# A sparse graph transformer on one core: twenty gathers of each of the last two layers issued during the end of the layer before

## Chip, core and metric

The kernel runs on one core of a Trainium2 chip. The metric is the device time of one launch in microseconds (us), as the median of three runs.

## The reference, cut to what matters

There are 3327 nodes of 256 features and a 0/1 adjacency of 3327 x 3327 with about 16 ones in a row. Layer 0 is one graph attention step; layers 1 to 3 are masked transformer layers of the same form with their own weights:

```python
qkv = layer_norm(x, g1, be1) @ w_qkv
q, k, v = ...                                   # 8 heads of 32
scores = einsum('nhd,mhd->hnm', q, k) * SCALE
scores = where(adj != 0, scores, -inf)
out = einsum('hnm,mhd->nhd', softmax(scores), v).reshape(n, 256)
x = x + out @ w_proj + b_proj
x = x + gelu(layer_norm(x, g2, be2) @ w1 + b1) @ w2 + b2     # 1024 wide
```

## The kernel before, in words

**Layer 0 and the lists.** Layer 0 reads the adjacency once (25 loads of 1.66 MB), sorts the nodes by their number of neighbours, largest first, and keeps for every node the list of its neighbours. The sorted nodes lie in 26 blocks of 128; block 0 has the nodes with the most neighbours. `CAPS` holds the list length of each block: 34 for block 0, 23 for block 1, 12, 12, 11, 10 and 9 for blocks 21 to 25; their sum is 430. `idx` holds the lists, `bias` a large negative number where a list has a place too many.

**A layer.** Keys and values of all nodes lie in DRAM as rows of 512 floats (`kv_dr`; in layer 1 a 513th number is the key's place in the sorted order, which `scores` copies into `idx` for the later layers). The blocks are worked off in `ORDER`: 24, 23, ..., 0, then 25. A block's list is cut into groups of up to four places (`cuts`). For each group:

- `gather` issues one indirect DMA a place on the POOL queue (L767): 128 rows, one for each node of the block, into a buffer (`slots`) of 4 rows of `SLW` floats. There are 12 buffers (`SLOTS`), used in turn.
- `scores` multiplies the keys by q (L781) and sums over each head (L782), on DVE. q stands in PSUM (`place_q`, ACT, L760).
- After a block's last group, `exps` makes the exponentials (L788 to L792), and beside the next block's groups `shares` (L798 to L800) and `values` follow: a DVE multiplication of the values by the shares (L812) and two PE transposes a place that add up in PSUM (L815); then ACT copies the sum to SBUF (L821).

**A tail.** When both blocks of a chunk (`CHUNKS`: 23 and 24, 21 and 22, ..., 1 and 2, then 0 alone, 25 alone) are done, `tail` runs as a generator, one step at a time: the projection (L666, L670), the addition to x (L673) and the variances on DVE; the power -1/2 on POOL (`powers`, L139, tiles rsig); the normalised rows on ACT (xn, L155), their transposes (pn on PE, fT on ACT); two halves of the feed-forward, each a wave of `w1` products (pu, L694), gelu on ACT (L698) and a wave of `w2` products (pd, L707); the second addition (L713). In layers 1 and 2 there follow the next layer's norm (rsig_h, nmu, xn, hT), its qkv products (L185, L190) and the writes of kv and q to DRAM (L729, L730, SP queue). A list `hidden` lets one tail at a time through the feed-forward.

**The order.** `layer` writes the order of all instructions out by hand (`manual_schedule`); each engine and each queue runs its own in that order. The layer is a sequence of turns, one for each group: gathers for up to `AHEAD` = 3 groups further on are issued while a buffer is free, then this group's scores, then `turn()` steps every tail on (twice in a turn of block 25), then some value groups of the block before (`part`; block 1's six are spread over block 0's nine turns by `goal`). After the last block come the remaining values and steps without gathers: I call that stretch the layer's ending. The next layer's first gather waits until all 26 blocks of kv have landed. In layer 3 there is no kv; `write` scatters finished blocks to the output from the POOL queue (L833), and each of these writes waits for the one before.

**A fallback.** After layer 3 a flag is computed from the lists; if it is set, `general` computes everything anew. For the inputs of these runs it is not set.

Of the kernel before, what the change touches and what calls it, by code (L numbers as in the profile page):

```python
# [50 lines left out]
SLW = 2 * D + 16  # L51
# [10 lines left out]
ORDER = list(range(NB - 2, -1, -1)) + [NB - 1]  # L62
CHUNKS = [ORDER[k:k + 2][::-1] for k in range(0, NB - 2, 2)] + [[0], [NB - 1]]


@with_exitstack
def kernel(ctx: ExitStack, tc: tile.TileContext, ins, out: bass.AP):
# [28 lines left out]
    pf = const.tile([P, NB], FP, name="permf")  # L96
    lists = ctx.enter_context(tc.tile_pool(name="lists", bufs=1))
# [140 lines left out]
    with ExitStack() as st:  # L238
# [70 lines left out]
        nc.vector.tensor_copy(pid, pid_i)  # L309
        tri = l0.tile([P, P], BF, name="tri")  # L310
# [205 lines left out]
        def order():  # L516
# [14 lines left out]
            nc.sync.dma_start(kv_dr[1][:, 2 * D:KVW].rearrange("(k p) o -> p (k o)", p=P), rank)  # L531
# [99 lines left out]
    with ExitStack() as st:  # L631
# [25 lines left out]
        def tail(L, w, wqn, blocks, oT):  # L657
# [69 lines left out]
            for j, b in enumerate(blocks):  # L727
                kv, q = qkv_rows(work, gen, wqn, hT[:, :, j * P:(j + 1) * P], L + 1, f"{L + 1}_{b}")
                nc.sync.dma_start(kv_dr[L + 1][b * P:(b + 1) * P, :], kv)  # L729
                nc.sync.dma_start(q_dr[L + 1][:, b, :], q)  # L730
                if j < n - 1:
                    yield 1

        def cuts(b):

            n = -(-CAPS[b] // SG)
            at = [CAPS[b] * k // n for k in range(n + 1)]
            return list(zip(at[:-1], at[1:]))

        class Attend:  # L740


            def __init__(self, L, b):
                self.L, self.b, self.tag, self.S = L, b, f"{L}_{b}", CAPS[b]
                self.cuts = cuts(b)
                self.tiles = []
                self.vdone = 0
                w = qws[ORDER.index(b) % 2]
# [3 lines left out]
            def load_q(self):  # L752
                if self.L == LAYERS[0]:
                    self.q = nodes_[self.b][:, D:2 * D]
                else:
                    self.q = work.tile([P, D], FP, tag="q", bufs=3, name=f"q_{self.tag}")
# [5 lines left out]
            def gather(self, g):  # L762
                a, z = self.cuts[g]
                t = slots.tile([P, SG, SLW], FP, tag="slot", name=f"sl_{self.tag}_{g}")
                w = KVW if self.L == LAYERS[0] else 2 * D
                for k in range(a, z):
                    nc.gpsimd.indirect_dma_start(  # L767
                        out=t[:, k - a, :w], out_offset=None, in_=kv_dr[self.L][:, :],
                        in_offset=bass.IndirectOffsetOnAxis(ap=idx[:, self.b, k:k + 1], axis=0))
                self.tiles.append(t)  # L770

            def scores(self, g):
                a, z = self.cuts[g]
                n = z - a
                if g == 0:
                    self.sc = work.tile([P, LW, HEADS], FP, tag="sc", name=f"sc_{self.tag}")
                if self.L == LAYERS[0]:

                    nc.scalar.copy(idx[:, self.b, a:z], self.tiles[g][:, :n, 2 * D])
                kq = self.tiles[g][:, :n, :D]  # L780
                nc.vector.tensor_mul(kq, kq, self.qp[:, None, :].to_broadcast([P, n, D]))  # L781
# [3 lines left out]
            def exps(self):  # L785
# [6 lines left out]
                nc.scalar.activation(scs, scs, AF.Exp, scale=SCALE)  # L792

# [11 lines left out]
            def values(self, oT, j):  # L805
# [7 lines left out]
                for k in range(n):  # L813
                    for c in range(2):
                        nc.tensor.matmul(self.po[:, c, :], t[:, k, D + c * P:D + (c + 1) * P], ident,  # L815
                                         is_transpose=True, start=False,
                                         stop=(a + k == self.S - 1 and c == 1))
                self.vdone += 1
# [28 lines left out]
        def layer(L):  # L847
# [31 lines left out]
            for k, a in enumerate(att):  # L879
# [3 lines left out]
                for g in range(n):  # L883
# [17 lines left out]
                    if k == NB - 1:  # L901
                        turn()
# [214 lines left out]
```

## Time and profile before

| | us |
|---|---|
| runs: median (lowest, highest) | 2878.28 (2872.93, 2891.91) |
| profiled execution, its own time | 2350.96 |
| its span, first to last instruction | 2349.1 |
| layer 0 and the lists, to the first gather | 0 to 417.8 |
| layer 1: first gather to end of last | 417.8 to 1012.1 |
| ending of layer 1 | 1012.1 to 1086.6 |
| layer 2: first gather to end of last | 1086.6 to 1649.9 |
| ending of layer 2 | 1649.9 to 1724.7 |
| layer 3: first gather to end of last | 1724.7 to 2285.4 |
| last output write starts | 2334.6 |

Mean TensorE clock granted: 0.802 of full speed. The profile is one execution; its times are from the span's start. PE is the matrix engine (PEld its weight loads), DVE the vector engine, ACT the scalar engine, POOL GpSimd, SP the queue of the plain DMAs. A row of a group names line, engine, operation, out<-in, count, busy time, mean ns of one, and the idle time before it with what ended it. A row in order of time names start, length, the instruction, and in brackets the engine's idle time before it and what ended that; "issue" means that nothing the profile shows was waited for.

### The profile page before, as it was taken

To read this page: it belongs to the slowest core of one execution; us is meant where nothing else is said; L and a number is where in the kernel's file an instruction comes from. 1 tells how busy PE (TensorE), PEld (TensorE's weight loads), DVE (VectorE), ACT (ScalarE), POOL (GpSimd) and SP (SyncE) were. 2 spreads that over 40 slices of the span, in tenths; PEclk is the share of its full clock that TensorE was granted. 3 is DMA by queue.
4 is the path that set the end of the run, shared out by engine and by line. 5 is a ranking of instruction groups with operands and counts; after the bars stand their busy time and mean duration, and the time that the engine had idled before them with its cause. 6 is when DMAs were issued, how large, how long until landed. Compare 5 with 4: busy or idle time off the path is not lost. (4 is left out here: it accounts for less than half of the span.)

```text
span 2349.1 us, 26111 instructions
## 1 busy us (share of the span) xinstructions
PE 1619.5 (69%) x8346; PEld 1278.3 (54%) x8346; DVE 1758.5 (75%) x3214; ACT 778.9 (33%) x1564; POOL 1430.9 (61%) x1614
## 2 busy tenths in 40 slices
PE   7676763258767778774578778777837767766666
PEld 6555642146645556553466566655625656554555
DVE  4876774699888888862888878778548888887772
ACT  3876751124333322222134332222321323211112
POOL 1222232777777776723777777767157777777772
PEclk9888886579877778887789877877967888767778
DMA  5767715777777777725777777767167777776761
GB/s 191 253 184 193 193 59 98 203 207 219 234 217 214 218 220 206 211 68 191 217 220 225 230 219 224 233 201 214 46 204 214 211 214 212 212 204 200 203 196 36
DMA packets 165083, 453.05 MB, mean 193 GB/s; under 512 B 37711, under 2 KB 64985, under 8 KB 161609
## 3 DMA queue, kind: packets, MB, share of 16 engines
q0 software_dynamic: 107104, 350.26, 51.8%
q1 hardware_dynamic: 56652, 98.53, 13.5%
q10 hardware_dynamic: 1180, 2.49, 0.4%
q8 instruction: 69, 1.13, 0.2%
q14 instruction: 78, 0.64, 0.1%
HBM read 410.86 MB, written 40.29 MB: 192 GB/s over the span
## 5 line engine op out<-in xcount | busy, mean ns | idle before, releaser
L767 POOL DMA_INDIRECT sl<-kv,idx x1290 | 1228.6, 952 | 410.4 <-issue 311.7
L815 PE MATMUL po<-ident,sl 128*128 128x128 f32 x2580 | 465.7, 344 | 505.2 <-DVE sl L812 479.3
L815 PEld LDWEIGHTS po<-ident,sl 128*128 128x128 f32 x2580 | 393.0, 179 | 568.4 <-DVE sl L812 557.0
L781 DVE TENSOR_TENSOR sl<-sl,qw 128x1024 f32<-128x1024 f32 (+1 forms) x354 | 396.4, 1120 | 170.9 <-DMA sl<-kv,idx 86.8
L782 DVE TENSOR_REDUCE sc<-sl 128x32 f32<-128x1024 f32 (+1 forms) x354 | 398.2, 1125 | 12.1
L812 DVE TENSOR_TENSOR sl<-sl,qw 128x1024 f32<-128x1024 f32 (+1 forms) x354 | 388.9, 1119 | 2.7
L694 PE MATMUL pu<-fT,w 128*128 128x256 f32 (+1 forms) x1344 | 297.7, 377 | 9.6 <-ACT fT L167 9.6
L707 PE MATMUL pd<-w,gT 128*128 128x256 f32 x1248 | 288.8, 384 | 0.9 <-ACT gT L698 0.9
L694 PEld LDWEIGHTS pu<-fT,w 128*128 128x128 f32 x1344 | 248.0, 198 | 42.8 <-ACT fT L167 12.1
L707 PEld LDWEIGHTS pd<-w,gT 128*128 128x128 f32 x1248 | 232.7, 191 | 38.4 <-ACT gT L698 4.8
L698 ACT ACTIVATE gT<-pu,pv 128x256 f32<-128x256 f32 (+1 forms) x336 | 133.1, 456 | 204.3 <-PE pu L694 203.2
L821 ACT COPY oT<-po 128x256 f32<-128x256 f32 x78 | 29.1, 373 | 466.9 <-PE po L815 466.3
L185 PE MATMUL pk<-wq,hT 128*128 128x512 f32 x312 | 170.0, 673 | 12.7 <-ACT hT L167 12.7
L713 DVE TENSOR_TENSOR x_sb<-x_sb,pd 128x512 f32<-128x512 f32 (+1 forms) x42 | 27.2, 647 | 185.9 <-PE pd L707 185.8
L610 DVE MAX8 cand<-abf 128x8 f32<-128x256 bf16 x338 | 118.2, 410 | 1.4 <-DMA node<-cand 1.1
L187 ACT COPY kvr<-pk 128x512 f32<-128x512 f32 x78 | 46.0, 590 | 191.9 <-PE pk L185 171.0
L185 PEld LDWEIGHTS pk<-wq,hT 128*128 128x128 f32 x312 | 62.3, 217 | 64.4 <-issue 41.3
L280 POOL MEMSET abf<- 128x1 bf16 x26 | 2.6, 103 | 149.8 <-DVE cand L610 86.3
L670 PE MATMUL pp<-w_proj,oT 128*128 128x256 f32 x312 | 89.7, 435 | 1.1 <-ACT oT L821 0.8
L600 ACT ACTIVATE aT<-pt 128x1024 bf16<-128x1024 bf16 x104 | 85.5, 874 | 8.1 <-PE pt L599 7.9
L190 PEld LDWEIGHTS pq<-wq,hT 128*128 128x128 f32 x312 | 61.6, 197 | 46.5 <-issue 38.4
L603 PE MATMUL pa<-hs,aT 128*128 128x193 bf16 x676 | 78.4, 270 | 8.0 <-ACT aT L600 7.5
(220 smaller groups left out, 1921.2 us busy)
## 6 DMA issues: line engine op xcount, KB each, us to landing
a<-in_adj_dram SPq DMA_DIRECT2D x25, 1663.5 KB
sl<-kv,idx POOLq DMA_INDIRECT x1290, 3.8
kv<-kvr SPq DMA_DIRECT2D x78, 256.0 KB
q<-qr SPq DMA_DIRECT2D x52, 128.0 KB
q<-q SPq DMA_DIRECT2D x52, 128.0 KB
w<-in_L_gnn_w_dram SPq DMA_DIRECT2D x6, 1024.0 KB
node<-x SPq DMA_DIRECT2D x26, 128.0 KB
node<-qr SPq DMA_DIRECT2D x26, 128.0 KB
```

The lines of the kernel that those rows point to most:

```text
L185: nc.tensor.matmul(pk, hT[:, c, :], wq[:, c, D:], start=(c == 0), stop=(c == 1))
L600: nc.scalar.activation(aT[:, k0:k0 + kn, :], pt[:, :kn, :], AF.Sign)
L610: nc.vector.max(out=cand[:, 8 * m:8 * m + 8], in_=ab3[:, m, :])
L670: nc.tensor.matmul(pp[:, j, :], oT[:, c, j * P:(j + 1) * P], w["w_proj"][:, c, :], start=False, stop=(c == 1 and j == n - 1))
L694: nc.tensor.matmul(pu[:, a, :n * P], w["w1"][:, c, f * P:(f + 1) * P], fT[:, c, :n * P], start=(c == 0), stop=(c == 1))
L698: nc.scalar.activation(gT[:, f0 + a, :n * P], pu[:, a, :n * P], AF.Gelu_apprx_tanh, bias=pv[:, L - 1, 8 + f:9 + f])
L707: nc.tensor.matmul(pd[:, j, :], gT[:, f, j * P:(j + 1) * P], w["w2"][:, h * FH + f, :], start=False, stop=(h == 1 and f == FH - 1 and j == ...
L767: nc.gpsimd.indirect_dma_start(out=t[:, k - a, :w], out_offset=None, in_=kv_dr[self.L][:, :], in_offset=bass.IndirectOffsetOnAxis(ap=idx[: ...
L781: nc.vector.tensor_mul(kq, kq, self.qp[:, None, :].to_broadcast([P, n, D]))
L782: nc.vector.tensor_reduce(self.sc[:, a:z, :], kq.rearrange("p s (h d) -> p s h d", h=HEADS), AX.X, ALU.add)
L812: nc.vector.tensor_mul(vv, vv, self.pw[:, a:z, :, None].to_broadcast([P, n, HEADS, HD]))
L815: nc.tensor.matmul(self.po[:, c, :], t[:, k, D + c * P:D + (c + 1) * P], ident, is_transpose=True, start=False, stop=(a + k == self.S - 1 ...
```

## The change

- The kv rows of layers 2 and 3 (and the places in the sorted order) are laid out anew: blocks 0, 1, 2 and 25 (`ENDING`), which are finished last, lie behind the other 22 (`AT`, `FIRM` = 22 x 128 rows).
- `resort`, in layer 1 only, sorts the lists of blocks 24, 23, 22 and 21 on DVE so that places among the 22 firm blocks come first. Their first 4, 4, 4 and 8 places (`BEFORE`, 20 in all, five groups) then touch firm rows alone. If a list has too few such neighbours, `beyond` sets the fallback's flag; for these inputs none has.
- `ahead` issues these 20 gathers of the next layer in the ending of layers 1 and 2, two at a step, after loading q of the four blocks; `ahead_scores` makes their scores there, with q from SBUF.
- The loop of the next layer leaves these groups out.
- Tails are stepped twice a turn beside block 0 also, and block 1's values go two groups a turn there.
- A gather may go when the buffer next in turn has been given back (`room`), in place of a count.
- A buffer row is 516 floats, not 528; the score tile is smaller; q has four buffers.

The diff, cut to its core:

```diff
-SLW = 2 * D + 16
+SLW = 2 * D + 4
+ENDING = [0, 1, 2, NB - 1]
+AT = {b: k for k, b in enumerate([b for b in range(NB) if b not in ENDING] + ENDING)}
+BEFORE = {24: 4, 23: 4, 22: 4, 21: 8}
+FIRM = (NB - len(ENDING)) * P
...
-                nc.sync.dma_start(kv_dr[L + 1][b * P:(b + 1) * P, :], kv)
+                nc.sync.dma_start(kv_dr[L + 1][AT[b] * P:(AT[b] + 1) * P, :], kv)
...
+        def room():
+            return given[0] < SLOTS or given[0] - SLOTS in back
...
             def scores(self, g):
...
+                    if self.b in BEFORE:
+                        if g == 0:
+                            self.kf = lists.tile([P, 16], FP, tag="kf", name=f"kf_{self.b}", bufs=2)
+                            nc.vector.memset(self.kf, -float(NP))
+                        nc.scalar.mul(self.kf[:, a:z], self.tiles[g][:, :n, 2 * D], -1.0)
+                    else:
+                        nc.scalar.copy(idx[:, self.b, a:z], self.tiles[g][:, :n, 2 * D])
                 kq = self.tiles[g][:, :n, :D]
-                nc.vector.tensor_mul(kq, kq, self.qp[:, None, :].to_broadcast([P, n, D]))
+                q = self.q if g < self.n0 else self.qp
+                nc.vector.tensor_mul(kq, kq, q[:, None, :].to_broadcast([P, n, D]))
...
+            def resort(self):
+                S, b, kf = self.S, self.b, self.kf
+                e = BEFORE[b]
+                j = list(BEFORE).index(b)
+                pad = lists.tile([P, 16], FP, tag="rpad", name=f"rpad_{b}", bufs=1)
+                ks = lists.tile([P, 16], FP, tag="ks", name=f"ks_{b}", bufs=1)
+                nc.vector.scalar_tensor_tensor(pad[:, :S], bias[:, b, :S], -1.0, over[:, :S], ALU.is_lt, ALU.mult)
+                nc.vector.tensor_add(kf[:, :S], kf[:, :S], pad[:, :S])
+                nc.vector.max(out=ks[:, :8], in_=kf)
+                nc.vector.match_replace(out=kf, in_to_replace=ks[:, :8], in_values=kf, imm_value=-float(NP))
+                nc.vector.max(out=ks[:, 8:], in_=kf)
+                nc.vector.tensor_scalar(pad, ks, 0.5, None, ALU.is_gt)
+                nc.vector.scalar_tensor_tensor(ks, ks, 0.5, ks, ALU.is_lt, ALU.mult)
+                nc.vector.tensor_scalar(bias[:, b, :S], pad[:, :S], NEG, None, ALU.mult)
+                nc.vector.scalar_tensor_tensor(kf, pad, owns[:, j:j + 1], ks, ALU.mult, ALU.add)
+                nc.vector.tensor_scalar(beyond[:, j:j + 1], kf[:, e - 1:e], 0.5 - FIRM, None, ALU.is_lt)
+                nc.vector.tensor_scalar(idx[:, b, e:S], kf[:, e:S], -1.0, None, ALU.mult)
+                nc.vector.tensor_scalar(idx[:, b, :e], kf[:, :e], -1.0, FIRM - 1.0, ALU.mult, ALU.min)
...
+        def ahead(L):
+            while (L - 1, CHUNKS[-4][0]) not in written:
+                yield
+            for a in atts[L][:len(BEFORE)]:
+                a.load_q()
+            for a, g in early(L):
+                while not room():
+                    yield
+                for k in range(0, SG, 2):
+                    a.gather(g, k, k + 2)
+                    yield
+                a.sent = g + 1
+
+        def ahead_scores(L):
+            for a, g in early(L):
+                while a.sent <= g:
+                    yield
+                for _ in range(3):
+                    yield
+                a.scores(g)
+                yield
...
-                    while sent < turns and held < SLOTS and sent - now <= AHEAD:
+                    while sent < turns and room() and sent - now <= AHEAD:
...
                     turn()
-                    if k == NB - 1:
+                    if k >= NB - 2:
                         turn()
...
-                        goal = max(g + 1, -(-len(before.cuts) * (g + 1) // max(n - 1, 1)))
+                        h = (g - a.n0 + 1) * (2 if k == NB - 2 else 1)
+                        goal = max(h, -(-len(before.cuts) * h // max(n - a.n0 - 1, 1)))
...
             before.shares()
+            pre = [ahead(L + 1), ahead_scores(L + 1)] if L < LAYERS[-1] else []
             while before.vdone < len(before.cuts):
                 part(before)
                 turn()
                 write(1)
+                for e in pre[:1]:
+                    next(e, None)
             while tails:
                 turn()
                 write(1)
+                for e in pre:
+                    next(e, None)
```

In the changed program the lines move: L767 becomes L807, L781 L830, L812 L881, L713 L732, L139 L150.

## The prediction

> **What bounds the kernel now.** I read the page first, then busy time by stage, then POOL's instructions in order of time.
>
> ```profile
> PE 1619.5 (69%) x8346; PEld 1278.3 (54%) x8346; DVE 1758.5 (75%) x3214; ACT 778.9 (33%) x1564; POOL 1430.9 (61%) x1614
> L767 POOL DMA_INDIRECT sl<-kv,idx x1290 | 1228.6, 952 | 410.4 <-issue 311.7
> L781 DVE TENSOR_TENSOR sl<-sl,qw 128x1024 f32<-128x1024 f32 (+1 forms) x354 | 396.4, 1120 | 170.9 <-DMA sl<-kv,idx 86.8
> ```
>
> By the shares DVE is busiest. But a gather (L767) is 952 ns on POOL, and before nearly each stands 0.30 us of "issue". The table by stage (columns PE, PEld, DVE, ACT, POOL, clock, DMA share, GB/s) splits the span into layer 0, layer 1, its ending, layer 2, its ending, layer 3, the end:
>
> ```profile
> 0.00:412.00 412.00, 273.45 (x2023) 210.36 (x2023) 271.67 (x874) 243.06 (x358) 100.43 (x202) 0.85 0.58 167
> 412.00:1013.00 601.00, 405.68 (x1864) 319.03 (x1864) 510.11 (x967) 181.81 (x480) 451.00 (x479) 0.78 0.74 215
> 1013.00:1086.00 73.00, 64.37 (x330) 48.36 (x330) 28.06 (x57) 28.18 (x68) 2.89 (x5) 0.95 0.11 36
> 1086.00:1650.00 564.00, 405.20 (x1864) 318.71 (x1864) 451.58 (x640) 160.72 (x317) 425.49 (x453) 0.80 0.76 225
> 1650.00:1724.00 74.00, 64.37 (x330) 48.38 (x330) 29.31 (x59) 27.91 (x65) 3.82 (x6) 0.95 0.11 39
> 1724.00:2285.00 561.00, 360.78 (x1672) 294.61 (x1673) 448.66 (x585) 121.96 (x238) 427.70 (x451) 0.75 0.73 213
> 2285.00:2349.00 64.00, 45.62 (x264) 38.84 (x263) 19.12 (x35) 15.24 (x38) 19.57 (x20) 0.87 0.14 44
> ```
>
> In layer 2, 430 gathers at 1.25 us are 537.5 of 564 us; the rest is 23 small powers (rsig, which push the next gather back 0.6 us each) and some 12 us of short waits, most of them late in the stage. POOL is the bound of each gathering stage, while DVE has 112 us to spare there. In the two endings POOL does almost nothing and PE is busy 64 of 73 us. POOL at the turn from layer 1 to 2:
>
> ```profile
> 1011.11 0.96 POOL L767 DMA_INDIRECT sl<-kv,idx  x1 [0.30 <-issue]
> 1012.09 0.74 POOL L139 TENSOR_TENSOR rsig_f<-rsig_f,mhalf 128x2 f32<-128x2 f32 x1
> 1039.12 0.55 POOL L139 TENSOR_TENSOR rsig_f<-rsig_f,mhalf 128x1 f32<-128x1 f32 x1 [26.30 <-DVE rsig_f L135]
> 1076.68 0.54 POOL L139 TENSOR_TENSOR rsig_h<-rsig_h,mhalf 128x1 f32<-128x1 f32 x1 [9.66 <-DVE rsig_h L135]
> 1086.61 1.03 POOL L767 DMA_INDIRECT sl<-kv,idx  x1 [9.39 <-DMA kv<-kvr]
> 1087.95 0.95 POOL L767 DMA_INDIRECT sl<-kv,idx  x1 [0.30 <-issue]
> 1089.20 0.95 POOL L767 DMA_INDIRECT sl<-kv,idx  x1 [0.30 <-issue]
> ```
>
> From the last gather's end T (1012.1) to the first of layer 2 is 74.5 us, ended by the last kv block's landing. Starts are 1.25 us apart (1087.95 to 1089.20).
>
> **The change, part by part.** All against the profiled execution (2350.96 us, span 2349.1).
>
> 1. *Twenty gathers leave the stream of layers 2 and 3.* 20 x 1.25 = 25.0 us a layer, 50.0 in all: POOL issues there without a wait. They go where POOL is idle 70 of 73 us; without that cover the 25 us would be back. In POOL's order (read from both programs) 2 stand ahead of rsig_f of block 0, 8 more ahead of rsig_f of block 25, 10 more ahead of the two rsig_h. The first waits for kv rows of blocks 3 and 4 (written long before) and for the PE transposes of block 0's first value group; SP gets 4 q loads (128 KB each) after the kv writes of blocks 1 and 2, and the later q loads stay behind the weights as now.
>
> 2. *Two steps a turn and two value groups a turn beside block 0.* Block 1's values end at block 0's third turn, not the eighth, so the tail of blocks 1 and 2 runs its feed-forward (4 waves of 3.6 us: rows L694, L707, 16 matmuls each, 3.62 and 3.72) before block 0's values. In the ending 14.5 us of PE go, and qkv of blocks 3 and 4 (2 x 2.9) with them. But the rsig_f of that tail stands on POOL ahead of the last 13 gathers, so it runs at T-16; its transposes on PE queue behind qkv of 3 and 4 (T-13 to T-11), and four waves end at about T+4. The L713 addition for it now stands on DVE before block 25's first scores, which before began at T+1: DVE begins them at about T+6.
>
> 3. *The ending after.* DVE from T+6: scores of 25 1.9, shares 1.3, values 5.2, scores 1.9, values 4.6: T+21. Transposes, copy and projection (0.9+0.4+1.4), then scores and exponentials still due on DVE, x_sb addition and statistics 1.2, rsig 0.55: T+26. Values of 25 (2.7) and nmu: T+29.5; xn, pn, fT 1.8: T+31. Feed-forward of block 0 takes 7.9 us and that of block 25 7.8 (layer 3's last rows: 2315.59 to 2323.46, 2324.19 to 2332.05), with 0.9 between: T+48. POOL meanwhile: first early gathers about T+11, held at rsig_f of 0 until T+26, 8 gathers to T+36, rsig_f of 25 just in time, 10 gathers to T+49, rsig_h of 0 (ready T+41) at T+49.5. DVE's nmu for it stands ahead of the last addition, which slips to T+50. From that addition to the first gather is now 11.4 us (1075.25 to 1086.61); an early score (2.4 us) stands in it, of which the rsig's trip hides 0.7: T+63. Against 74.5: 11 us less, 22 for both. Late next is the rsig_h behind the gathers, 2 us.
>
> 4. *Early scores.* 5 groups x (1.22+1.22) = 12.2 us of DVE move into the ending, where DVE is busy 28 of 73; they cost only the 1.7 us counted.
>
> 5. *resort in layer 1.* 4 x 13 small DVE operations; no row has them, the nearest are 128x16 ones (L229 to L234, 175 to 235 ns) and MAX8 on 104 columns (270): about 2.7 us a block, 11 us. DVE idles 7 us between 440 and 500 and 19 between 540 and 700, and POOL may run groups ahead in 12 buffers. Between 0 and 6 (all that does not fit the first idle time, were the buffers no cover); I take 1, near zero because POOL shows no wait there.
>
> 6. *The end.* The first five of the 16 last output writes follow each other 2.67 us apart (each waits for the one before); blocks 0 and 25 no longer stand behind the feed-forward of 1 and 2, but rsig_f of 25 stands on POOL behind 9 writes and 7 follow it: last write about 2329, not 2334.55: 5.5 us less.
>
> Sum: 50 + 22 + 5.5 - 1 = 76.5 us: 2350.96 - 76.5 = 2274.5.
>
> The median of the runs is 2878.28, 527 us above the profiled execution; no view says where these lie. I take them as a constant: 2878.28 - 76.5 = **2802 us**. If everything is stretched by 1.224, the gain is 94 us (2785).
>
> **Two rules weighed.** First the trace: while DVE ran L788 (two inputs in SBUF, 1011.60 to 1012.04), the gather over it took 0.96 us, against 0.95 alone. The Trainium skill ("SBUF — State Buffer", Who interferes with whom) says such an instruction contends with a GpSimd instruction that reads SBUF, as a gather does for its indices; the early scores multiply by q in SBUF instead of PSUM. By the row the cost is 0; by the rule up to 5 x 1.22 = 6 us an ending: gain 64, not 76. I take the row.
>
> Second: TensorE's clock was 0.95 in the endings, where PE is nearly full, and 0.50 to 0.60 around 1740 and 1000 to 1020, where it is not. The skill ("TensorE: Matmul & The Clock Gate", Part 1) halves the clock after an idle window of some 3.4 us. The new ending has about 44 us of PE work in 63, with a gap of up to 6 us before block 0's feed-forward. By the row at 1.00 the waves cost what I wrote; if both ran cold, 15.7 us more an ending: gain 45.
>
> **Rivals.**
> - *The ending gives nothing* (PE cold, or the feed-forward beside block 0 holds DVE longer): For: block 0's stage is already 16.8 of 20 us of PE at 980 to 1000. Against: at 0.98 clock. About -6 in place of +11 each: gain 50 - 12 + 2 - 1 = 39: 2839.
> - *The 527 us lie in the gathers or in everything*: 40 x 0.41 us more, or x 1.224: 2785.
> - *The stream does not shorten*: the buffers rotate in order, and early groups hold 5 of 12; if POOL waits for them at layer 2's start, 25 us come back as waits. For: the gather after block 22's first early group is put off a turn. Against: 3 turns of lookahead, about 13 us. Only endings remain, 26.5: 2852.
> - *Slower: the buffer's row shrinks from 528 to 516 words.* Rows of 2048 bytes then start at multiples of 16 bytes, not 64, in SBUF. No row shows this. DMA is 0.76 busy in 1.25 us, 0.95 us a gather, so it decides from 1.32 times that. The nearest row is layer 1, whose rows of 2052 bytes at an odd pitch in DRAM went at the same 1.25 us. Were the transfer 1.45 times as long, 1.38 us on 1250 gathers: +160 - 76: 2962. Break-even is at 1.31 us a gather.
>
> **How the numbers follow.** Main case 0.52 (2802, its own range 2785 to 2820); weak ending 0.19 (2839); scaled 0.12 (2785); stream not shortened 0.09 (2852); slower 0.08 (2962). Range 2755 to 2858: below by the scaled case with an ending that gives 10 us more, above by the fourth; it leaves out the slower case and some tails. A percent is 28.8 us and about what this kernel's measurement can tell from no change: faster is below 2849.5. Faster 0.52 + 0.12 + 0.19 less a little: 0.82; within 1% 0.10; slower 0.08.
>
> **What would show it.** Right: the layers' first gathers after the tails still 1.25 us apart; layer 2 from its first to last late gather some 538 us; 20 gathers with gaps inside the ending; from T to the first late gather 60 to 66 us; no feed-forward wave of 128x256 outputs in the ending; DVE waiting at L732 before block 25. Wrong: gathers further apart than 1.27 us; POOL waiting for PE at the start of layer 2; an ending clock below 0.8; resort rows after which POOL waits in layer 1.

## The result and the profile after

The changed kernel takes 2867.98 us (median of 12 runs, 2855.42 to 2878.18), the kernel before 2877.16 (12 runs, 2859.12 to 2898.12). The ratio is 0.9959, 95% interval 0.9937 to 0.9981: 9 us faster, clear of zero but an eighth of the 76 us forecast. The forecast was 2802 with a range of 2755 to 2858; 2868 lies outside it.

One fact is needed to read what follows: the profiled execution of before, 2350.96 us, is unlike its runs. The experiments were measured in five sets, here A to E, each with the kernel before beside it. The kernel before took 2856 to 2877 us (medians) in A, B and C, and 2353 to 2354 in D and E. I call these the long and the short kind of execution. The results carry the chip numbers 8, 7, 13, 9 and 7: B, of the long kind, and E, of the short kind, have the same one. The profiled execution of after, 2874 us, is of the long kind. So before and after are compared here kind by kind: before (2351) with the changed kernel profiled in E (2324), and the kernel before profiled again in A (2881) with after (2874).

The changed kernel's page, the lines that answer to those of before (every line number of the old code after `cuts` is higher now: L767 is L807, L713 is L732, L673 is L692, L139 is L150, L821 is L891):

```profile
PE 1716.4 (60%) x8346; PEld 1336.3 (47%) x8346; DVE 1760.1 (61%) x3280; ACT 778.1 (27%) x1564; POOL 1438.2 (50%) x1615
L807 POOL DMA_INDIRECT sl<-kv,idx x1290 | 1233.6, 956 | 613.0 <-issue 381.8
```

A gather still costs 956 ns, but POOL's idle time before gathers is 613 us, where it was 410 in the profile of before and is 562 in the kernel before in A. The table by stage of the changed kernel in E (PE, PEld, DVE, ACT, POOL, clock, DMA share, GB/s; split into the same stages as the prediction's):

```profile
0.00:415.00 415.00, 278.98 (x2023) 213.26 (x2023) 273.55 (x883) 244.61 (x359) 103.11 (x207) 0.83 0.55 167
415.00:1023.00 608.00, 414.87 (x1896) 323.31 (x1897) 517.56 (x1026) 186.11 (x488) 447.24 (x476) 0.79 0.72 212
1023.00:1095.00 72.00, 58.79 (x299) 45.52 (x298) 39.66 (x64) 25.89 (x62) 23.85 (x25) 0.94 0.37 112
1095.00:1648.00 553.00, 418.21 (x1897) 325.21 (x1898) 440.99 (x634) 163.51 (x326) 406.99 (x433) 0.81 0.73 221
1648.00:1720.00 72.00, 58.44 (x299) 45.31 (x297) 39.66 (x64) 25.48 (x57) 23.97 (x26) 0.94 0.36 113
1720.00:2256.00 536.00, 364.00 (x1719) 297.78 (x1720) 429.44 (x568) 122.76 (x244) 409.51 (x432) 0.77 0.72 212
2256.00:2324.00 68.00, 36.40 (x217) 30.57 (x215) 24.63 (x41) 12.12 (x30) 18.41 (x18) 0.83 0.12 40
```

The endings are 72 us where the forecast had 63, and PE is still busy 58.8 us in them (64.4 before, 44 forecast): the feed-forward of blocks 1 and 2 has not left. For finer cuts I took the starts of the gathers from POOL's rows. "To last 44" runs from a layer's first late gather to its 44th from the end (the last of block 1), "last 44" from there to the last gather, "ending" from there to the next layer's first late gather. All in us:

| | before (2351) | early gathers, E | both edits, E | changed, E | before, A | changed (2874) |
|---|---|---|---|---|---|---|
| layer 1 to last 44 | 536.0 | 540.0 | 537.1 | 540.1 | 707.0 | 718.1 |
| last 44 | 57.4 | 57.3 | 66.5 | 66.5 | 70.0 | 78.9 |
| ending | 75.5 | 75.6 | 73.3 | 73.5 | 76.3 | 92.5 |
| layer 2 to last 44 | 505.8 | 485.3 | 505.7 | 485.2 | 669.4 | 641.0 |
| last 44 | 56.6 | 56.6 | 66.1 | 66.1 | 62.0 | 77.5 |
| ending | 75.7 | 75.7 | 72.9 | 73.2 | 77.6 | 80.4 |
| layer 3 to last 44 | 502.4 | 477.1 | 502.5 | 477.2 | 649.0 | 607.0 |
| last 44 | 57.4 | 57.4 | 57.9 | 57.9 | 66.5 | 78.6 |
| end | 64.7 | 64.3 | 68.5 | 69.0 | 77.5 | 75.0 |

"Early gathers" is the changed kernel without the two edits beside block 0, "both edits" those two edits alone (early_again and ending_again below). The columns of E add up nearly exactly: what the gathers save stands in the two long rows of layers 2 and 3, what the edits cost stands in the rows of the last 44 gathers and the end. In A the three long rows are longer than in the profile of before by 171, 164 and 147 us, the last-44 rows and the end by 5 to 13 each, the endings by 1 to 2: that is where the 527 us are.

### The profile page after: what moved, and what is told of

It reads as the page before. It is cut to its first block, busy times and chain, and to the rows that moved or that the text cites. A ratio compares the mean times of both kernels' runs of the same rounds, so it can differ in the third digit from the quotient of the medians.

```text
span 2872.7 us, 26164 instructions
## 1 busy us (share of the span) xinstructions
PE 1716.4 (60%) x8346; PEld 1336.3 (47%) x8346; DVE 1760.1 (61%) x3280; ACT 778.1 (27%) x1564; POOL 1438.2 (50%) x1615
## 4 chain that ended last, share of the span: by engine, by line
PE 34%; DVE 17%; issue 16%; another core or an unknown queue 16%; ACT 6%; DMA 6%; POOL 4%; DVEq 0%; ACTq 0%; POOLq 0%; SPq 0%
PE pd L726 8%; PE pu L713 8%; PE po L884 6%; PE pk L196 4%; DVE sl L881 4%; DVE sl L830 3%; PE pp L689 2%; POOL sl L807 2%; DVE sc L831 2%; DMA node<-qr 2%; PE pq L201 2%; DMA sl<-kv,idx 1%; DMA kv<-kvr 1%; DMA out_dram<-x_sb,perm 1%
## 5 line engine op out<-in xcount | busy, mean ns | idle before, releaser
L807 POOL DMA_INDIRECT sl<-kv,idx x1290 | 1233.6, 956 | 613.0 <-issue 381.8
L830 DVE TENSOR_TENSOR sl<-sl,qw 128x1024 f32<-128x1024 f32 (+1 forms) x344 | 384.0, 1116 | 62.6 <-DMA sl<-kv,idx 31.6
L713 PE MATMUL pu<-fT,w 128*128 128x256 f32 (+1 forms) x1344 | 336.0, 409 | 129.9 <-issue 86.6
L726 PE MATMUL pd<-w,gT 128*128 128x256 f32 x1248 | 327.7, 420 | 115.1 <-ACT gT L717 103.5
L881 DVE TENSOR_TENSOR sl<-sl,qw 128x1024 f32<-128x1024 f32 (+1 forms) x354 | 387.9, 1119 | 6.9 <-issue 3.1
L713 PEld LDWEIGHTS pu<-fT,w 128*128 128x128 f32 x1344 | 273.1, 219 | 178.9 <-issue 92.6
L726 PEld LDWEIGHTS pd<-w,gT 128*128 128x128 f32 x1248 | 257.2, 212 | 173.8 <-ACT gT L717 116.1
L732 DVE TENSOR_TENSOR x_sb<-x_sb,pd 128x512 f32<-128x512 f32 (+1 forms) x42 | 27.3, 649 | 434.7 <-PE pd L726 343.7
L891 ACT COPY oT<-po 128x256 f32<-128x256 f32 x78 | 29.1, 373 | 648.9 <-remote 274.8
L150 POOL TENSOR_TENSOR rsig_f<-rsig_f,mhalf 128x2 f32<-128x2 f32 (+1 forms) x42 | 29.2, 695 | 291.2 <-DVE rsig_f L146 275.6
L692 DVE TENSOR_TENSOR x_sb<-x_sb,pp 128x512 f32<-128x512 f32 (+1 forms) x42 | 27.3, 649 | 228.9 <-PE pp L689 202.1
L178 ACT ACTIVATE fT<-pn_f,pv 128x256 f32<-128x256 f32 (+1 forms) x84 | 41.6, 546 | 233.2 <-remote 138.0
L150 POOL TENSOR_TENSOR rsig_h<-rsig_h,mhalf 128x2 f32<-128x2 f32 (+1 forms) x28 | 23.3, 832 | 162.4 <-DVE rsig_h L146 161.3
L176 PE MATMUL pn_f<-ident,xn_f 128*128 128x128 f32 x156 | 40.2, 387 | 103.6 <-ACT xn_f L166 81.7
L867 DVE TENSOR_REDUCE sm<-sc 128x8 f32<-128x120 f32 (+11 forms) x78 | 29.8, 382 | 113.6 <-ACT sc L841 87.8
```

The source lines that it names most:

```text
L713: nc.tensor.matmul(pu[:, a, :n * P], w["w1"][:, c, f * P:(f + 1) * P], fT[:, c, :n * P], start=(c == 0), stop=(c == 1))
L726: nc.tensor.matmul(pd[:, j, :], gT[:, f, j * P:(j + 1) * P], w["w2"][:, h * FH + f, :], start=False, stop=(h == 1 and f == FH - 1 and j == ...
L807: nc.gpsimd.indirect_dma_start(out=t[:, k - a, :w], out_offset=None, in_=rows, in_offset=bass.IndirectOffsetOnAxis(ap=idx[:, self.b, k:k + ...
L830: nc.vector.tensor_mul(kq, kq, q[:, None, :].to_broadcast([P, n, D]))
L881: nc.vector.tensor_mul(vv, vv, self.pw[:, a:z, :, None].to_broadcast([P, n, HEADS, HD]))
```

## The experiments

**The halves alone, and the kernel before once more (set A).** Both halves are cut from the diff. The early gathers alone put the old stepping back into the changed kernel:

```diff
-                    if k >= NB - 2:
+                    if k == NB - 1:
                         turn()
-                        h = (g - a.n0 + 1) * (2 if k == NB - 2 else 1)
+                        h = g - a.n0 + 1
```

The edits alone put `k >= NB - 2` and the factor 2 into the kernel before.

> The kernel before, unchanged, profiled once more. Theory P (the profile that the prediction used shows the ordinary execution, and POOL's gathers at 1.25 us each set the pace): the profiled execution takes about 2351 us again, about 38 gathers in every 50 us of a gathering stage. Theory W (the ordinary execution is another one, in which signals between engines come late and the gathering stages are set by waits of PE, ACT and DVE on one another): about 2860 to 2900 us, 25 to 30 gathers in 50 us, single waits of 10 to 30 us on ACT and DVE, as in the profile of the changed kernel.

> The kernel before with two steps a turn and two value groups a turn beside block 0, and no early gathers. Theory P: the endings fall by some 14 us each from the feed-forward that leaves them, and the end by 5.5: 2877 - 22 to 33 = 2844 to 2855. Theory W: the steps moved into the gathering stage are steps of the chains that set that stage, so most of it comes back there: 2865 to 2880.

> The changed kernel with one step and one value group a turn beside block 0, as before: only the twenty early gathers a layer, the re-sorted lists and the narrower buffer stay. Theory P: 50 us leave the two streams, some 4 to 10 us of them come back in the endings: 2827 to 2840. Theory W: gathers off POOL's stream are worth little while the stage is set by waits: 2865 to 2885.

Measured: before 2880.66; the edits alone 1.0094 (1.0061 to 1.0126), slower; the early gathers alone 0.9799 (0.9765 to 0.9834), 2822 against 2877. The gathers gave the 50 us forecast for them (54). The edits were 29 us slower, worse than either theory had it, so they cost about what they were to gain. What the long kind of execution looks like, in the kernel before in A (timeline; in brackets the idle time before):

```profile
492.09 1.97 PE L815 MATMUL po<-ident,sl 128*128 128x128 f32 x8 [1.54 <-DVE sl L812]
504.14 0.37 ACT L821 COPY oT<-po 128x256 f32<-128x256 f32 x1 [23.19 <-remote]
504.61 3.75 PE L670 MATMUL pp<-w_proj,oT 128*128 128x256 f32 x8 [10.02 <-issue]
510.59 0.72 POOL L139 TENSOR_TENSOR rsig_f<-rsig_f,mhalf 128x2 f32<-128x2 f32 x1 [15.77 <-DVE rsig_f L135]
```

PE's transposes end at 494.06; the ACT copy that waits for them alone starts 10.1 us later, "remote" meaning that no end of an instruction fits the signal. PE's recorded signals for three groups that ended at 488.66, 490.55 and 494.06 stand at 498.34, 504.02 and 504.11. Behind the copy waits the projection, behind that DVE's addition, behind that POOL's power, and behind that the gathers. In the profile of before no wait over 5 us on ACT, DVE or PE is put down to "remote"; here there are 43, 710 us together, all but one of them on ACT.

**Does POOL set the pace (set A)?** One gather of each group of layers 2 and 3 is replaced:

```diff
+                if self.L > LAYERS[0]:
+                    nc.sync.dma_start(t[:, 0, :w], kv_dr[self.L][self.b * P:(self.b + 1) * P, :w])
-                for k in range(a, z):
+                for k in range(a + (self.L > LAYERS[0]), z):
```

> The kernel before, but in layers 2 and 3 the first row of every group of slots is filled by a plain load of 128 consecutive rows from SP's queue in place of a gather (the attention then uses wrong rows there; bytes and all other work stay). 236 of 860 gathers leave POOL. Theory P: 236 x 1.25 = 295 us less, about 2582. Theory W: POOL has slack, 0 to 80 us less: 2797 to 2877. If DMA transport sets the pace, not POOL's issuing: no change or slower, 2870 to 2920.

Measured: 0.9187 (0.9142 to 0.9233), 2641 against 2877. 236 us for 236 gathers, 1.0 us each, between the two theories and nearer to P: even in the long kind a gather that leaves POOL is worth most of its 1.25 us. How much of that is POOL's own time, and how much is signals that come sooner with fewer gathers (see the kernel without gathers below), this run does not tell.

**Which of the two edits costs (set B)?** In the changed kernel, one of the two is put back (the first or the second hunk above).

> The changed kernel with two value groups a turn beside block 0, but one step a turn there. The early gathers alone measured 2822. Theory E (two steps a turn leave PE's four feed-forward waves, 14.5 us, half the gathering time to run in, so DVE stands at the addition L732 for them and POOL's small powers stand behind it): harmless, 2816 to 2832. Rival V (the value multiplies, 1.2 us of DVE each, two a turn, push block 0's scores back): 2840 to 2850.

> The changed kernel with two steps a turn beside block 0, but one value group a turn. Theory E: this is the part that costs: 2840 to 2860. Rival V: harmless, 2816 to 2832.

Measured: two value groups a turn alone 0.9980 (0.9959 to 1.0001), two steps a turn alone 0.9989 (0.9969 to 1.0009). Against 0.980 without either (set A), each costs nearly 2% by itself, and both together 1.6%. Theories E and V, which each blamed one edit, are both refuted. The trace shows why they don't add: each alone already puts one more of POOL's powers ahead of the last gathers while DVE still stands. In layer 1 two value groups alone move the power of blocks 1 and 2 from behind the last gather to ahead of the last six. Two steps alone move it ahead of the last three, and that of blocks 3 and 4 from ahead of the last six to ahead of the last 17; POOL waits 9.4 and 3.7 us at these two. Two value groups alone, layer 1:

```profile
1182.54 0.69 DVE L732 TENSOR_TENSOR x_sb<-x_sb,pd 128x512 f32<-128x512 f32 x1 [18.71 <-PE pd L726]
1184.79 0.71 POOL L150 TENSOR_TENSOR rsig_h<-rsig_h,mhalf 128x2 f32<-128x2 f32 x1 [9.20 <-DVE rsig_h L146]
1187.02 0.70 POOL L150 TENSOR_TENSOR rsig_f<-rsig_f,mhalf 128x2 f32<-128x2 f32 x1 [1.52 <-DVE rsig_f L146]
```

**Is it DVE's standing at that addition (set C)?** The addition L732 of the tails of blocks 3, 4 and 1, 2 is put four (or three) turns later:

```diff
-            yield 1
+            yield 4 if b0 in (1, 3) else 1
             nc.vector.tensor_add(xi, xi, pd[:, :n, :])
```

> The changed kernel, but the addition of the feed-forward (L732) of the pairs 3, 4 and 1, 2 is issued four turns after its last wave instead of one, 1.5 groups later. Theory E2 (what the two edits of block 0's stage cost is DVE's standing at L732 for PE's waves, 10 to 22 us each time, with POOL's small powers held behind it): the stages of block 0, 77.5 to 78.9 us in the changed kernel, come back to 66 to 72, ratio to before 0.978 to 0.988. Rival (the wait moves on to the power or to the next projection): ratio 0.992 to 1.0.

> The changed kernel with one step a turn and two value groups a turn beside block 0 (0.998 of before), and the same addition of the pairs 3, 4 and 1, 2 issued three turns after its last wave instead of one. Theory E2: 0.980 to 0.988. Rival: 0.994 to 1.002.

Measured: 0.9874 (0.9835 to 0.9913) and 0.9980 (0.9960 to 1.0000). In the first, half of the loss comes back, but not in the rows of the last 44 gathers as E2 had it (78.9, 77.5 and 78.6 became 77.6, 75.8 and 79.4). Against the profile of the changed kernel, this one is shorter by 10 us in the ending of layer 1 (92.5 in the changed kernel, 82.3 here) and by 16 in layer 2 up to the last 44 gathers (641.0 and 625.3). In that ending the granted clock was 0.82 in the changed kernel and 0.92 here, with PE busy 69 and 61 us, so these 10 us need not be the edit's. In the second the wait moved one addition on, as the rival had it:

```profile
1193.25 0.69 DVE L692 TENSOR_TENSOR x_sb<-x_sb,pp 128x512 f32<-128x512 f32 x1 [15.73 <-PE pp L689]
1195.49 0.71 POOL L150 TENSOR_TENSOR rsig_f<-rsig_f,mhalf 128x2 f32<-128x2 f32 x1 [7.44 <-DVE rsig_f L146]
```

**Where the 527 us lie, and whether they can be had (sets B and C).** From the early gathers alone, the addition of the projection three turns late, in all layers and then in layer 3 alone:

```diff
-            yield 1
+            yield 3 if L == LAYERS[-1] else 1
             nc.vector.tensor_add(xi, xi, pp[:, :n, :])
```

> The early gathers alone, and in every tail the addition of the projection (L692) waits three turns instead of one after its matmuls are issued; statistics and powers shift with it. In the profiles of the ordinary execution DVE stands at that addition for 202 us in 22 waits, and POOL at the power behind it for 276 us in 37. Theory W (these waits, about 15 us at every pair of blocks, are most of the 527 us between the profile that the prediction used and the runs): two turns, some 10 us, are taken from each of some 36 waits: 150 to 320 us less than 2822, so 2500 to 2670. Rival (the stages are limited by the throughput of POOL or PE, and the wait only moves to the next step of the tail): 2790 to 2840.

> The early gathers alone (0.980 of before), and in layer 3 alone the addition of the projection waits three turns instead of one. In all layers this moved nothing in sum, but its layer 3 was 40 us shorter from first gather to the start of block 0 and its endings 9 to 10 us longer. If those are two effects, the gain without the loss: 0.965 to 0.972. If the 40 us were chance: 0.977 to 0.983.

Measured: 0.9805 (0.9759 to 0.9850) in all layers, so no gain over 0.9799; 0.9701 (0.9652 to 0.9750) in layer 3 alone, 2772 against 2856, the best right version in the long kind. In all layers the waits moved: early gathers alone first, then with the late addition everywhere (group, sum, times, longest):

```profile
POOL rsig_f L150 <- DVE rsig_f L146: 256.9, 33, 16.4
DVE sm L867 <- ACT sc L841: 78.8, 7, 16.6
POOL sl L807 <- PE po L884: 61.8, 21, 10.8
```

```profile
DVE sm L867 <- ACT sc L841: 169.9, 17, 18.7
POOL sl L807 <- PE po L884: 118.8, 30, 21.6
POOL rsig_f L150 <- DVE rsig_f L146: 90.2, 25, 12.1
```

167 us left POOL's first power; 148 us came up at DVE's wait for the exponentials, which stand on ACT behind copies and gelus that wait for PE, and at POOL's wait for buffers that PE has yet to read. Another 45 us came up at POOL's second power, rsig_h (109 to 154). Only layer 3 kept the gain (572.5 and 574.2 us up to the last 44 gathers, where the early gathers alone took 614.3 in A). Its tails have no second power; that this is the reason was not tested.

**Do the signals come late through bytes or through gathers (sets B and C)?** In one kernel each gather fetches half as much, in the other there are none. Both then work on wrong rows, with the same instructions otherwise. The edits, cut to their core:

```diff
-                w = KVW if self.L == LAYERS[0] else 2 * D
+                w = KVW if self.L == LAYERS[0] else D
```

```diff
-                    nc.gpsimd.indirect_dma_start(
-                        out=t[:, k - a, :w], out_offset=None, in_=kv_dr[self.L][:, :],
-                        in_offset=bass.IndirectOffsetOnAxis(ap=idx[:, self.b, k:k + 1], axis=0))
+                    nc.sync.dma_start(t[:, k - a, :w], kv_dr[self.L][self.b * P:(self.b + 1) * P, :w])
```

(The second only in layers 2 and 3.)

> The kernel before, but each gather of layers 2 and 3 fetches 256 words a row in place of 512 (the values are left out, the attention multiplies its key rows in their place); number of gathers and all other instructions stay. If the late signals of the ordinary execution come from the gathers' bytes on the DMA engines: 100 to 250 us less, 2630 to 2780. If they come from the number of gathers or have nothing to do with DMA: 2850 to 2885.

> The kernel before, with every gather of layers 2 and 3 replaced by a plain load of 128 consecutive rows of the same size on SP's queue (wrong rows; bytes and all other work stay; POOL keeps only its small powers there). If signals between engines come late only while POOL issues gathers: stages of layers 2 and 3 of 450 to 520 us instead of 715 to 731, no wait over 10 us put down to an unknown source, 2400 to 2480 in all. If they come late whatever issues the loads: stages over 600 us, above 2620.

Measured: 1.0030 (1.0008 to 1.0052) with half the bytes, so not the bytes; 0.8639 (0.8596 to 0.8682), 2474 us, without gathers in layers 2 and 3. There all "remote" waits over 5 us lie in layer 1, which kept its gathers. Layers 2 and 3 of that kernel, from the first group's scores to the last's:

```profile
1281.00:1843.00 562.00, 421.60 (x1921) 328.66 (x1921) 466.60 (x660) 163.88 (x325) 16.01 (x23) 0.80 0.63 220
1911.00:2425.00 514.00, 359.21 (x1726) 294.77 (x1727) 451.22 (x594) 121.86 (x239) 23.47 (x27) 0.78 0.67 228
```

562 and 514 us where the kernel before in A has 731 and 715 from first gather to last. So in the long kind the signals are late only in stretches where POOL issues gathers. Gathers alone do not make them late: in D and E POOL issues as many.

**Do the edits lose only through late signals (sets D and E)?** The same two edits in the kernel without gathers in layers 2 and 3, and the side parts of the change alone (`self.n0 = 0`, no edits):

> The kernel with plain loads for all gathers of layers 2 and 3 (wrong rows; 0.864 of before, signals on time in those layers), with two steps a turn and two value groups a turn beside block 0. Theory S (the two edits lose because signals come late in the gathering stage, and each step put there meets one more late signal): with signals on time they do what the prediction said in layers 2 and 3, the ending of layer 2 and the end 5 to 11 us shorter each; layer 1 and its ending lose some 10; in sum 0.858 to 0.864. Theory Q (they lose because PE's four waves of 3.6 us and DVE's work do not fit beside block 0, whatever the signals): the stages of layers 2 and 3 get 8 to 15 us longer as in the gathering kernel, in sum 0.870 to 0.876.

> The changed kernel without early gathers and with one step and one value group a turn beside block 0: what stays is the re-sorted lists of four blocks in layer 1, the narrower buffer row (516 words), the moved table rows, the groups cut at the early length and the q loads of four blocks in the ending. The prediction gave these 1 us together (slower rival: 160 us from the buffer's row). Theory: they cost next to nothing, ratio 0.998 to 1.006, and so the early gathers alone are worth 1.9 to 2.3 per cent. Rival: they cost 10 to 30 us, 1.004 to 1.010, and the gathers' worth is that much higher than 54 us.

Measured: in D the kernel before takes 2353 us. The side parts cost 1.0008 (0.9992 to 1.0024): 2 us, not clear of zero. The other kernel's ratio, 0.9872 (0.9843 to 0.9900), has no partner without the edits in this set, but its trace has one in the kernel without gathers of set C: layers 2 and 3 of both are without gathers and without late signals. By the starts of the score multiplications on DVE (L784), the first 99 groups of a layer take the same in both (477.6 and 477.5 us; 432.4 and 432.1). From the 100th group to the last the edits add 23.9 us in layer 2 and 14.1 in layer 3; from there to the next layer's first, or to the end, they take off 16.8 and 5.5. So they lose 7 and 8 us even where POOL has no gathers for them to hold up. Set E then tested them with gathers:

> The two edits without early gathers, once more. With signals on time, theory S (they lose only because signals come late): the prediction's 22 to 33 us less, ratio 0.986 to 0.991. Theory Q: 0 to 15 us more, 1.000 to 1.006. If the signals are late again: 1.009.

> The early gathers without the two edits, once more. With signals on time, prediction's steps: 50 less from the stream and 3 to 8 us back in the endings: 2306 to 2311, ratio 0.980 to 0.982. If the signals are late again: 0.980 too.

> The changed kernel, unchanged, once more. In the last two measurements the kernel before itself took 2353 us, as in the profile that the prediction used, where on three other chips it took 2857 to 2877: the late signals belong to the chip or the moment. If they are absent again, the prediction's sum can be put to the test in the execution that it was made for. Prediction's steps (50 from the stream, 22 from the endings, 5.5 from the end): 2353 - 76 = 2277, ratio 0.967. Theory Q (the edits beside block 0 do not fit, whatever the signals): 2300 to 2320, 0.978 to 0.986. If the signals are late again: 0.996.

> The early gathers, with the addition of the projection three turns late in layer 3 alone (0.970 where signals were late). With signals on time POOL hardly waits for that power (67 us in all before), so the 27 us that it gained there should be gone: ratio 0.978 to 0.983, as the early gathers alone. If the signals are late again: 0.970.

Measured, with signals on time: the edits alone 1.0080 (1.0054 to 1.0106), 19 us slower; the early gathers 0.9830 (0.9803 to 0.9856), 42 us faster; the whole change 0.9912 (0.9887 to 0.9938), 24 us faster; the late addition in layer 3 0.9825 (0.9798 to 0.9852), no more than the early gathers, as expected. Theory S is refuted: the edits lose with signals on time too, and by more than the ranges of theory Q allowed (15 us and 0.986). The prediction's sum, 76 us, was 24 in the very kind of execution that it was worked out from.

## Why the prediction was wrong

**Step 1, the stream: right.** 50 us forecast. In E 20.5 (505.8 to 485.3) and 25.3 (502.4 to 477.1) left the streams; in layer 2 the missing 4.5 us are two waits of 3.6 and 1.4 at a power further on. In A the early gathers gave 54 us. The gathers found their cover: in E the endings did not get longer for them (75.6 and 75.7 against 75.5 and 75.7).

**Steps 2 and 3: the failure.** The direction was wrong: forecast 22 us less, and the two edits alone cost 19 us in E (with step 6) and 29 in A. Two terms were mis-sized.

*"the rsig_f of that tail stands on POOL ahead of the last 13 gathers, so it runs at T-16"*, costed at nothing. It ran at T-17, but neither it nor the power before it was ready when POOL came to it. The changed kernel in E, POOL and DVE beside block 0:

```profile
988.62 0.95 POOL L807 DMA_INDIRECT sl<-kv,idx  x1 [1.97 <-issue]
995.70 0.69 DVE L732 TENSOR_TENSOR x_sb<-x_sb,pd 128x512 f32<-128x512 f32 x1 [7.91 <-PE pd L726]
997.95 0.71 POOL L150 TENSOR_TENSOR rsig_h<-rsig_h,mhalf 128x2 f32<-128x2 f32 x1 [4.60 <-DVE rsig_h L146]
1005.93 0.71 POOL L150 TENSOR_TENSOR rsig_f<-rsig_f,mhalf 128x2 f32<-128x2 f32 x1 [2.28 <-DVE rsig_f L146]
```

The same before:

```profile
994.83 0.69 DVE L713 TENSOR_TENSOR x_sb<-x_sb,pd 128x512 f32<-128x512 f32 x1 [4.54 <-PE pd L707]
1003.81 0.74 POOL L139 TENSOR_TENSOR rsig_h<-rsig_h,mhalf 128x2 f32<-128x2 f32 x1
1012.09 0.74 POOL L139 TENSOR_TENSOR rsig_f<-rsig_f,mhalf 128x2 f32<-128x2 f32 x1
```

Before, POOL met both powers without a wait. With two steps a turn the power of blocks 3 and 4 moves from behind the 38th of the last 44 gathers to behind the 27th, some 14 us sooner at 1.25 us each. Its input does not come sooner by as much: from the first of the 44 gathers to DVE's addition for blocks 3 and 4 it is 41.1 us before and 40.2 after. PE is busy without a break from 979.15 to 995.66, with that pair's four waves of 3.6 to 3.7 us and transposes of value groups between them. POOL then stands 4.6 and 2.3 us at the two powers, and 2.0 us before a gather ahead of them (its cause is not in the row): 8.9 us, of the 9.1 and 9.5 us of the table.

*"its transposes on PE queue behind qkv of 3 and 4 (T-13 to T-11), and four waves end at about T+4"*. T is 1022.88 here.

```profile
1010.04 0.15 DVE L162 SCALAR_TENSOR_TENSOR nmu_f<-mv_f,rsig_f 128x2 f32<-128x2 f32 x1
1010.32 3.78 PE L196 MATMUL pk<-wq,hT 128*128 128x512 f32 x4 [0.66 <-ACT hT L178]
1015.07 1.88 PE L196 MATMUL pk<-wq,hT 128*128 128x512 f32 x4
1016.78 1.03 PE L201 MATMUL pq<-wq,hT 128*128 128x256 f32 x4
1017.89 0.37 ACT L203 COPY qr<-pq 128x256 f32<-128x256 f32 x1 [0.28 <-PE pq L201]
1018.16 1.09 ACT L166 ACTIVATE xn_f<-x_sb,nmu_f,rsig_f 128x256 f32<-128x256 f32 x2
1020.40 5.43 PE L713 MATMUL pu<-fT,w 128*128 128x256 f32 x16 [0.66 <-ACT fT L178]
1036.81 0.69 DVE L732 TENSOR_TENSOR x_sb<-x_sb,pd 128x512 f32<-128x512 f32 x1 [17.85 <-PE pd L726]
```

The qkv of blocks 3 and 4 took PE from 1010.32 to 1017.81: 7.5 us, where I wrote 2 (T-13 to T-11), although the sentence before has them at 2 x 2.9. That is the larger part. nmu_f is ready at 1010.04, but xn_f stands on ACT behind the four copies of that kv and q, which I had not looked at; for this PE waits 1.0 us more before the transposes. The first wave starts at T-2.5 instead of T-10.5, and the four take 16.3 us, not 14.5 (the first one 5.4). So DVE, standing at L732, goes on at T+14, not T+4. Everything after it is late by the same amount and otherwise as forecast: the power of block 0 at T+35 (26 forecast), its second at T+60 (49.5), the first late gather at T+72.6 (63). The waves did not leave the ending: PE's work in it fell by 5.6 us, about that qkv, and not by the 20 of waves and qkv together; the ending fell by 2.0 and 2.5, not by 11.

Forecast for steps 2 and 3: -22. Measured in E: 2 x 9.3 - 4.5 = +14.

**Step 4, early scores: right**, hidden: 12 us more DVE in the ending and no time for it. **Step 5, resort:** 1 forecast, 4 in the stage of layer 1 (536.0 to 540.0), inside the bound of 6; with the other side parts 2 us in the runs, not clear of zero. **Step 6, the end:** -5.5 forecast, +4.3 measured (64.7 to 69.0): DVE stands 7.5 us at L732 for blocks 1 and 2 there too, until 4 us after the last gather's start, and block 0's power follows 23.9 us after that start instead of 17.0.

In E the sum is then -46 (gathers) + 4 + 14 + 4 = -24, as the runs say. Of the 52 us that separate this from -76, 36 lie in steps 2 and 3, 10 in step 6, 4 in step 1 and 3 in step 5.

**The constant of 527 us: wrong, and no harm to the gathers' part.** It is not outside the kernel's work, as I took it, nor spread evenly over everything: it lies in the gathering stages, in waits behind late signals. In A the gathers give 54 us instead of 42 and the edits cost 29 instead of 19. Together they should then leave 25 us, and the changed kernel has 9: in the long kind the halves do not simply add. Part of it shows in layer 1's ending of the changed kernel, 92.5 us long, where it was 80.9 with the early gathers alone and 72.8 with the edits alone: DVE stands 22 us at L732 there, and the clock was 0.82 with PE busy 69.4 us (in layer 2's ending 0.94 and 58.6). Why the clock fell in that one is open.

**The rules weighed.** Over each whole ending in E the clock was 0.94, as the row had it. But the qkv of blocks 3 and 4 and the first wave do not lie there: they lie between T-13 and T+3, where the prediction itself names a clock of 0.50 to 0.60 before (1000 to 1020). The same stretch after (PE, PEld, DVE, ACT, POOL, clock, DMA share, GB/s):

```profile
1008.00:1014.00 6.00, 4.86 (x9) 2.19 (x10) 5.90 (x7) 2.03 (x5) 4.61 (x5) 0.50 0.69 185
1022.00:1024.00 2.00, 2.00 (x7) 1.53 (x6) 0.00 (x0) 0.62 (x2) 0.88 (x1) 0.50 0.77 286
```

In the first stretch the keys and values of the first of the two blocks took 3.78 us, those of the second, later, 1.88, and the q 1.33 and 1.03; in the second stretch the first wave took 5.43 instead of 3.62. That is 4.0 of the 10 us by which DVE goes on late, and I had priced these instructions by rows at a clock of 1.00. The Trainium skill ("TensorE: Matmul & The Clock Gate", Part 1) gives an idle window of about 3.4 us as what halves the clock. The first stretch agrees: PE is idle 4.83 us up to 1008.48. The second does not: in the 3.4 us before it PE was busy 1.8 us and idle for no more than 1.0 at a time.

Of the 20 early gathers in layer 1's ending two took longer than 1.02 us, 1.11 and 1.46, and both began while an early score multiplied; that is 0.7 us, in favour of the rule on two inputs in SBUF ("SBUF — State Buffer", Who interferes with whom), but a tenth of the 6 us that I had drawn from it. Gathers that began before the multiplication kept their 0.96 us.

**The rivals.** "The ending gives nothing" named two of the causes, feed-forward beside block 0 that holds DVE and a cold PE, and priced them at 6 us a layer; in E it was 7 (9.3 in the last 44 gathers less 2.3 in the ending). No rival had the end 4.3 us longer. Nor did any have the long kind's 9 us: 2868 lies between "the stream does not shorten" (2852) and the kernel before, and the stream did shorten. The slower rival, the buffer's row, was refuted: 956 ns a gather, and 1.0008 for the side parts.

## What to carry to other kernels

Taking work off a gap-free queue and giving it to the same queue's idle stretch pays what the rows say (42 to 54 us of 50), signals late or not. Issuing the steps of a dependent chain sooner in fixed queues does not make their inputs sooner: walk every queue that the chain crosses, give each step its length at the clock of the stretch it moves into, and ask of each moved instruction when its input is made, before costing its wait at nothing. And when a profiled execution is 18% shorter than every timed run, it shows another kind of execution: profile again before the working, not after it.

## What the runs showed of the hardware

- The same kernel took 2353 and 2354 us in two sets and 2856 to 2877 in three others, with the same durations of single instructions (a gather 952 and 955 ns). The difference is waits between engines. In the long kind signals were recorded late (three of PE's, shown above, 9.7 to 13.5 us after the end of the work). In the kernel before in A 37 to 40% of the signals of PE, ACT and DVE together are missing from the record in the three gathering stages, and at most one in layer 0 and in the endings, where POOL issues few or no gathers. In layers 2 and 3 of the kernel without gathers there, none is missing (2033 of 2033).
- It does not follow the gathers' bytes (1.003 with half of them).
- What makes an execution long was not found. It does not go with the chip number: sets B and E have the same number, and there the kernel before took 2857 and 2354 us. If that number names one and the same chip, the kind changes with time; whether it does, the results do not say. Nor do the runs tell whether the recording has a part in it.
- The granted clock fell to 0.50 at 1021.3 in the changed kernel in E after 3.4 us in which PE was busy 1.8, with no idle stretch over 1.0 us; the wave then running took 5.43 us instead of 3.62.
